# Long convolution: x turned one slot later; output projection of sublayer A with its bias as three bfloat16 rows

## The chip, the cores and the metric

The kernel runs on one core of a Trainium2 chip. The metric is the device time of one execution in microseconds (us); lower is better. The core has a matrix engine (TensorE, PE in the profile, with its weight loads as PEld), a vector engine (VectorE, DVE), a scalar engine (ScalarE, ACT), a general engine (GpSimd, POOL) and a queue that issues most transfers (SyncE, SP). Each works through its own instructions in order; semaphores tie them together.

## The reference, cut to what matters

The reference is a small network of two layers over x, 4096 rows (two sequences of 2048) of 256 numbers. Each sublayer normalizes x and adds its result to it. Eight follow each other: a scan (sublayer A), a router with slots, a doubling recurrence (sublayer B), the router again, a long convolution (sublayer C), a ternary feed-forward, attention (sublayer D), the feed-forward again.

```python
# sublayer A, behind its scan over 2048 steps
y = y * jax.nn.silu(z)
return y @ W_out + b_out
# sublayer C: 512 channels, a filter of 1024 taps each
x = _silu(xc)                       # xc: a causal filter of 4 taps over the input projection
x_f = jnp.fft.rfft(x, n=n); k_f = jnp.fft.rfft(k_ssm, n=n)
y = jnp.fft.irfft(x_f * k_f[None], n=n)[..., :Lq]
y = y + x * D_skip[None, :, None]
y = y * _silu(z)
return jnp.einsum('bhl,dh->bld', y, W_out)
```

## The kernel before

**Sublayer A** (`sublayer_a`) runs in three stages. `scan_tables` loads x in 32 tiles (`sa_xi`, L182), normalizes them and makes the tables of the scan. `scan` is the loop over 2048 steps (L410 to L488). Then comes the output projection: for each of 32 tiles of 128 rows a multiplication on DVE (L570), a bias matmul (L572: a row of ones against the row `b_out`, both f32 and one partition high), two f32 matmuls over the halves of the 256 channels (L574), and an addition to the resident x on DVE (`add_to_x`, L156). PSUM has four buffers for these products. `load_x` (L583) brings x into SBUF in eight transfers of 512 KB. The order of the instructions here is set by a scheduler, which may move them ahead on their queue when they wait for nothing and their tile's place in SBUF is free. The weights of the router, which follow, are loaded into the place of sublayer A's tiles.

**`bias_rows`** (L825) exists in the kernel before and is used by sublayer B and by the feed-forward. It splits an f32 row into three bf16 rows whose sum is the row, and puts them into the first three partitions of a tile of zeros 128 partitions high:

```python
t = pool.tile([P, n], BF16, name=name, tag=name)
V.memset(t, 0.0)
...
for k in range(3):
    piece = pool.tile([1, n], BF16, ...)
    V.tensor_copy(piece, rest)
    if k < 2:
        V.tensor_tensor(rest, rest, piece, ALU.subtract)
    nc.sync.dma_start(out=t[k : k + 1], in_=piece)
```

A matmul of a bf16 tile of ones (128 by 128) with such a tile adds the bias to every row.

**Sublayer C** (`sublayer_c`) handles its 512 channels in four blocks of 128 (e = 0 to 3). A block has 32 slots, and a slot convolves four channels (`convolve`, L1185: 72 small matmuls against a Toeplitz table). The order in this loop is written out by hand and kept. Four slots (r = 0 to 3) make a group, and a group does three things side by side:

- every slot: `load_toep` (L1109, SP) loads the table of two slots ahead into one of three buffers, which the slot before must have left; `fill_toep` fills up the next slot's table with two copies on DVE (L1117, L1119) and two on ACT (L1118, L1120); then `convolve` runs on PE.
- blocks 0 to 2 prepare the next block's input, 512 columns per group: `x_project` (slot 0, PE), `x_first` (slot 0: a copy on ACT, two instructions on DVE), `x_rest` (slot 1, two on DVE), `x_silu` (slot 2, L1164 on ACT, and a transfer by POOL), `x_turn` (slot 3, L1171: four transposes on PE, ahead of the slot's convolution), `x_keep` (slot 3, L1175: a copy on DVE, behind the slot's fill).
- blocks 1 to 3 finish the block before: `leave` (every block, slot 0), `y_load` (slot 0, POOL), `y_gate` (slot 1, PE), `y_silu` (slot 1, ACT), `y_join` (slot 2, L1220 and L1221 on DVE), `y_project` (slot 3, L1229: eight f32 instructions on PE, behind x_turn and ahead of the convolution), `y_add` (slot 3, L1237 on DVE).

Of the kernel before, what the change touches and what calls it, by code (L numbers as in the profile page):

```python
# [23 lines left out]
P = 128  # L24
B, S, D = 2, 2048, 256
# [27 lines left out]
BF16 = mybir.dt.bfloat16  # L53
# [6 lines left out]
def new(pool, shape, name, **kw):  # L60
    return pool.tile(list(shape), F32, name=name, tag=name, **kw)


class Kernel:
# [486 lines left out]
    def sublayer_a(self):  # L551
        tc, nc = self.tc, self.nc
        with ExitStack() as c:
            dp = c.enter_context(tc.tile_pool(name="a_dram", bufs=1, space=DRAM))
            kp = c.enter_context(tc.tile_pool(name="a_keep", bufs=1))
            tabd = dp.tile([96, NT], F32, name="tabd", tag="tabd")
            dtd = dp.tile([4, NT + TG, 64], F32, name="dtd", tag="dtd")
            dxd = dp.tile([4, NT + TG, 64], F32, name="dxd", tag="dxd")
            zs = new(kp, [P, 2, NT], "zs")
            y = new(kp, [P, 2, NT], "y")  # L560
            self.scan_tables(zs, dtd, dxd, tabd)
            self.scan(y, dtd, dxd, tabd)
            self.open_x()
            self.load_x(self.a["x"])
            wo = self.load(kp, "A_W_out", pat="(k p) n -> p k n", p=P)
            bo = self.load_row(kp, "A_b_out")
            pp = c.enter_context(tc.tile_pool(name="a_ps", bufs=4, space=PSUM))
            for i in range(NI):
                ts = slice(i * P, (i + 1) * P)
                nc.vector.tensor_tensor(zs[:, :, ts], zs[:, :, ts], y[:, :, ts], ALU.mult)  # L570
                ps = new(pp, [P, D], "ps_o")
                nc.tensor.matmul(ps, self.ones1, bo, start=True, stop=False)  # L572
                for k in range(2):
                    nc.tensor.matmul(ps, zs[:, k, ts], wo[:, k, :], start=False, stop=k == 1)  # L574
                self.add_to_x(i, ps)
# [496 lines left out]
    def sublayer_c(self):  # L1072
# [7 lines left out]
        tc, nc = self.tc, self.nc  # L1080
# [4 lines left out]
        with ExitStack() as c:  # L1085
# [3 lines left out]
            kp = c.enter_context(tc.tile_pool(name="c_k", bufs=1))  # L1089
# [14 lines left out]
            def load_toep(s):  # L1104
                e, g = s // 32, s % 32
                t = toeps[s] = new(kb, [P, 4, W], "toep")
                for r in range(2):
                    first = kr.offset + (e * P + 4 * g + 2 * r) * KREV
                    nc.sync.dma_start(  # L1109
                        out=t[r * (P - Q) : r * (P - Q) + Q, 2 * r : 2 * r + 2],  # L1110
                        in_=bass.AP(kr.tensor, first, [[1, Q], [KREV, 2], [1, W]]),
                    )

            def fill_toep(s):
                t = toeps[s]
                a, b = t[:, 0:2], t[:, 2:4]
                V.tensor_copy(a[Q : 2 * Q, :, 0 : W - Q], a[0:Q, :, Q:W])  # L1117
                A.copy(b[2 * Q : 3 * Q, :, Q:W], b[3 * Q : P, :, 0 : W - Q])  # L1118
                V.tensor_copy(a[2 * Q : P, :, 0 : W - 3 * Q], a[0 : 2 * Q, :, 2 * Q : W - Q])  # L1119
                A.copy(b[0 : 2 * Q, :, 3 * Q : W], b[2 * Q : P, :, Q : W - 2 * Q])  # L1120
# [13 lines left out]
            def x_project(e, ch):  # L1134
                ps = held["x"] = new(pp, [P, CH], "ps")
                for k in range(2):
                    nc.tensor.matmul(
                        ps, wi[:, k, e * P : (e + 1) * P], xT[:, k, ch * CH : (ch + 1) * CH],
                        start=k == 0, stop=k == 1,
                    )  # L1140
# [26 lines left out]
            def x_turn():  # L1167

                ps = held["t"] = new(pt, [P, 4, P], "ps_t")
                for j in range(4):  # L1170
                    nc.tensor.transpose(ps[:, j, :], held["xs"][:, j * P : (j + 1) * P], self.ident)  # L1171

            def x_keep(e, ch):
                b, i0 = ch // 4, ch % 4 * 4
                V.tensor_copy(  # L1175
                    xring[e % 2][:, :, TAPS + i0 : TAPS + i0 + 4, b], held["t"].rearrange("p j c -> p c j")
                )

            def convolve(s, ps):
                e, g = s // 32, s % 32  # L1180
                x, t = xring[e % 2], toeps.pop(s)
                for m in range(TAPS + 1):
                    for j in range(4):
                        lo = L_CONV - m * P + j // 2 * (P - Q)
                        nc.tensor.matmul(  # L1185
                            ps[j * 32 : (j + 1) * 32, g % 4, :],
                            x[:, 4 * g + j, TAPS - m : TAPS - m + NB, :].rearrange("p i b -> p (i b)"),
                            t[:, j, lo : lo + P], start=m == 0, stop=m == TAPS,
                        )

            def leave(s, ps):

                ys = new(tp, [P, 4, P], "c_ys")
                A.copy(ys, ps[:, :, ::-1])
                G.dma_start(
                    out=yd[4 * s : 4 * s + 16].rearrange("(s j) i b t -> (j i b) s t", j=4), in_=ys
                )


            def y_load(e, ch):  # L1200
                b, i0 = ch // 4, ch % 4 * 4
                yc, xs = held["yc"], held["yx"] = new(tp, [P, CH], "c_yc"), new(tp, [P, CH], "c_xs")
                G.dma_start(out=yc.rearrange("p (i t) -> p i t", t=P), in_=yd[e * P : (e + 1) * P, i0 : i0 + 4, b])
                G.dma_start(out=xs, in_=xd[e * P : (e + 1) * P, ch * CH : (ch + 1) * CH])

            def y_gate(e, ch):
                ps = held["z"] = new(pp, [P, CH], "ps")
                z0 = E * P + e * P
                for k in range(2):
                    nc.tensor.matmul(  # L1210
                        ps, wi[:, k, z0 : z0 + P], xT[:, k, ch * CH : (ch + 1) * CH], start=k == 0, stop=k == 1
                    )

            def y_silu():
                sz = held["sz"] = new(tp, [P, CH], "c_acc")
                A.activation(sz, held["z"], AF.Silu)
# [6 lines left out]
            def y_project(e):  # L1223
                yc = held["yc"]
                held["o"] = []
                for j0 in range(0, 4, 2):
                    ps = new(po, [P, 2, D], "ps_o")
                    for j in (j0, j0 + 1):
                        nc.tensor.matmul(  # L1229
                            ps[:, j - j0], yc[:, j * P : (j + 1) * P], wo[:, e, :], start=True, stop=True  # L1230
                        )
                    held["o"].append(ps)
# [18 lines left out]
            fill_toep(0)  # L1251
            x_turn()
            x_keep(0, NCH - 1)
            out = None
            for s in range(32 * E):
                e, q, r = s // 32, s % 32 // 4, s % 4
                more, done = e + 1 < E, e > 0
                if s + 2 < 32 * E:
                    load_toep(s + 2)
                if r == 0:  # L1260
                    before, out = out, new(pc, [P, 4, P], "ps_c")
                    if more:
                        x_project(e + 1, q)
                elif r == 1 and done:
                    y_gate(e - 1, q)
                elif r == 3:
                    if more:
                        x_turn()
                    if done:
                        y_project(e - 1)  # L1270
                if s + 1 < 32 * E:
                    fill_toep(s + 1)
                convolve(s, out)
                if r == 0:
                    if before is not None:
                        leave(s - 4, before)
                    if done:
                        y_load(e - 1, q)
                    if more:
                        x_first(e + 1, q)  # L1280
                elif r == 1:
                    if done:
                        y_silu()
                    if more:
                        x_rest(e + 1)
                elif r == 2:
                    if more:
                        x_silu(e + 1, q)
                    if done:
                        y_join(e - 1)  # L1290
                else:
                    if more:
                        x_keep(e + 1, q)
                    if done:
                        y_add(q)
            leave(32 * E - 4, out)
# [473 lines left out]
```

## Time and profile before

| | |
|---|---|
| time, median of 3 runs (range) | 13714.66 us (13710.65 to 13725.5) |
| the profiled execution's own time | 13713.61 us |
| its span, first to last instruction | 13711.9 us |
| busy: PE, DVE, ACT, POOL | 5477.8, 10653.5, 9294.0, 460.9 us |
| output projection of sublayer A | 10040.7 to 10142.1 us |
| convolution loop of sublayer C | 11039.8 to 11738.7 us |
| mean granted clock of PE | 0.609 of full speed |

The page gives busy times by engine, the span in 40 slices of 343 us, and the costliest groups of instructions, each with the idle time before it and what ended that. The timeline gives single instructions with start and length in us from the span's start; what stands in brackets is the idle time of the engine just before and who ended it. PEclk is the share of full speed that PE's clock was granted.

### The profile page before, as it was taken

How to read it: one execution, taken by the hardware profiler on the slowest of the kernel's cores; microseconds unless marked ns; L12 is line 12 of the kernel's file. 1: busy time of each engine (PE TensorE's matmuls, PEld its weight loads, DVE VectorE, ACT ScalarE, POOL GpSimd, SP SyncE). 2: the span in 40 equal slices, each digit the busy share in tenths (PEclk: the TensorE clock that was granted, in tenths of full speed). 3: DMA queues.
4: the chain of work that ended last, by engine and by line, in shares of the span. 5: the costliest groups of instructions: out<-in, count | busy, mean ns of one | idle time of the engine just before them, and what ended most of it. 6: DMA issues, size and time to landing. Idle time of an engine off the chain costs nothing. (4 is left out here: it accounts for less than half of the span.)

```text
span 13711.9 us, 263042 instructions
## 1 busy us (share of the span) xinstructions
PE 5477.8 (40%) x66344; PEld 3762.0 (27%) x66344; DVE 10653.5 (78%) x65491; ACT 9294.0 (68%) x45234; POOL 460.9 (3%) x528
## 2 busy tenths in 40 slices
PE   4222222222222222222222222222269867778888
PEld 2111111111111111111111111111135545644445
DVE  6888888888888888888888888888857677655555
ACT  3777777777777777777777777777735478534444
POOL 0000000000000000000000000000000001131110
PEclk6555555555555555555555555555559888889999
DMA  3000000000000000000000000000000045242210
GB/s 81 14 14 17 14 17 15 17 16 15 17 14 17 14 17 14 17 14 17 14 17 17 14 16 15 17 14 17 14 13 4 7 134 155 73 94 34 35 31 19
DMA packets 320440, 382.28 MB, mean 28 GB/s; under 512 B 207074, under 2 KB 230697, under 8 KB 317876
## 3 DMA queue, kind: packets, MB, share of 16 engines
q1 hardware_dynamic: 299444, 322.01, 10.2%
q0 software_dynamic: 17408, 42.75, 1.0%
q8 instruction: 533, 8.73, 0.3%
q14 instruction: 1007, 8.25, 0.2%
q10 hardware_dynamic: 2048, 0.53, 0.0%
HBM read 307.96 MB, written 52.46 MB: 26 GB/s over the span
## 5 line engine op out<-in xcount | busy, mean ns | idle before, releaser
L410 PE MATMUL hc<-hs,mean 128*32 128x2 f32 x16384 | 586.1, 203 | 7096.9 <-DVE hs L480 7033.2
L410 PEld LDWEIGHTS hc<-hs,mean 128*32 128x32 f32 x16384 | 410.6, 140 | 7308.9 <-DVE hs L480 7244.7
L475 DVE TENSOR_TENSOR p<-p,ir 128x64 f32<-128x64 f32 x4096 | 737.4, 221 | 1062.9 <-ACT ir L463 1062.9
L459 ACT ACTIVATE lm<-m 128x64 f32<-128x64 f32 x2048 | 466.2, 228 | 1210.2 <-DVE m L451 1210.2
L493 PE MATMUL yps<-cs,hist 128*64 128x8 f32 x8192 | 1224.9, 259 | 13.0 <-DVE hs L480 13.0
L391 ACT ACTIVATE bx<-dx,tc 128x64 f32<-128x64 f32 x4098 | 1169.4, 332 | 0.1
L1594 ACT ACTIVATE d_p<-ps_e 128x512 f32<-128x512 f32 (+3 forms) x1280 | 599.5, 537 | 754.2 <-PE ps_o L1575 534.8
L493 PEld LDWEIGHTS yps<-cs,hist 128*64 128x64 f32 x8192 | 1033.1, 218 | 45.1 <-DVE hs L480 13.4
L418 ACT ACTIVATE sq<-hc 128x2 f32<-128x2 f32 x2048 | 352.9, 172 | 795.2 <-PE hc L410 795.2
L480 DVE CUSTOM_DVE_ANT_0 hist<-p,sg 128x64 f32<-128x64 f32 x4096 | 761.0, 222 | 23.0 <-ACT rm L470 4.2
L477 DVE SCALAR_TENSOR_TENSOR p<-e,p 128x64 f32<-128x64 f32 x4096 | 738.1, 221 | 9.9 <-ACT sg L469 7.8
L442 DVE TENSOR_TENSOR p<-p,fac 128x64 f32<-128x64 f32 x4096 | 737.4, 221 | 8.9 <-DVE p L437 6.6
L444 DVE TENSOR_TENSOR p<-p,bx 128x64 f32<-128x64 f32 x4096 | 722.2, 218 | 2.6
L439 ACT ACTIVATE fac<-ngd,ci 128x64 f32<-128x64 f32 x2048 | 711.8, 348 | 1.0 <-DVE p L436 1.0
L436 DVE SCALAR_TENSOR_TENSOR p<-hist,ea 128x64 f32<-128x64 f32 x2048 | 459.7, 224 | 323.3 <-ACT ea L429 323.3
L429 ACT ACTIVATE ea<-ex 128x64 f32<-128x64 f32 x2048 | 524.3, 256 | 99.6 <-DVE ex L424 7.0
L1587 PE MATMUL ps_e<-d_qt,d_kt 128*128 128x512 f32 (+3 forms) x1280 | 556.4, 444 | 43.0 <-ACT d_p L1594 34.6
L472 ACT ACTIVATE ld<-e 128x64 f32<-128x64 f32 x2048 | 548.0, 268 | 0.0
L473 ACT ACTIVATE k<-rm 128x64 f32<-128x64 f32 x2048 | 545.0, 266 | 0.0
L410 PE MATMUL hd<-hs,mean 128*32 128x2 f32 x16384 | 543.7, 193 | 0.0
L1544 PE MATMUL ps_m<-d_kt,d_qt 128*128 128x512 f32 (+3 forms) x1280 | 499.3, 436 | 101.3 <-DVE d_part L1549 40.3
L432 PE MATMUL hd<-ident,ci 128*1 128x1 f32 x4096 | 386.7, 163 | 357.2 <-DVE ex L424 303.4
(453 smaller groups left out, 22720.5 us busy)
## 6 DMA issues: line engine op xcount, KB each, us to landing
toep<-in_C_krev SPq DMA_DIRECT2D x256, 312.0 KB, 5.5
ng<-dtd SPq DMA_DIRECT2D x258, 256.0 KB, 3.4
dx<-dxd SPq DMA_DIRECT2D x258, 256.0 KB, 3.9
d_kt<-d_kd SPq DMA_DIRECT2D x128, 128.0 KB, 4.1
d_qt<-d_qd SPq DMA_DIRECT2D x128, 128.0 KB, 3.7
y<-ys SPq DMA_DIRECT2D x512, 8.0 KB, 1.9
c_xd<-c_xs POOLq DMA_DIRECT2D x32, 256.0 KB, 2.6
c_yd<-c_ys POOLq DMA_DIRECT2D x32, 256.0 KB, 4.3
```

Source lines behind the costliest of these rows:

```text
L391: A.activation(bx[o][:, k2], tg[j][2][:, k], AF.Identity, scale=tg[j][0][:, k2, k : k + 1], bias=0.0 if k2 else SMALL,)
L410: nc.tensor.matmul(out[r : r + 32], mean[:, r : r + 32], hs[i], start=True, stop=True)
L439: A.activation(fac, ngd, AF.Exp, scale=ci)
L442: V.tensor_tensor(p[:, k2], p[:, k2], fac, ALU.mult)
L444: V.tensor_tensor(p[:, k2], p[:, k2], bx[o][:, k2], ALU.add)
L472: A.activation(ld, e, AF.Ln, scale=-1.0, bias=1.0)
L475: V.tensor_tensor(p[:, k2], p[:, k2], ir, ALU.mult)
L477: V.scalar_tensor_tensor(p[:, k2], e, -1.0, p[:, k2], ALU.add, ALU.mult)
L480: V.tensor_tensor_reduce(out=hn[:, k2], in0=p[:, k2], in1=sg, scale=-1.0, scalar=0.0 if k2 else J * SMALL, op0=ALU.mult, op1=ALU.add, accu ...
L493: nc.tensor.matmul(yps[:, k, :], hist[g][:, k, k2], tg[g][3][:, k2, k], start=k2 == 0, stop=k2 == 1)
L1587: nc.tensor.matmul(s[:, q0:], ks[kt // 4][:, hh, kt % 4 * P : (kt % 4 + 1) * P], q[:, hh, q0:], start=True, stop=not diag,)
L1594: A.activation(pr[:, q0:], s[:, q0:], AF.Exp, scale=0.25)
```

## The change

Two edits, apart from each other.

In `sublayer_a` the bias is made into three bf16 rows by `bias_rows` ahead of the scan, together with a bf16 tile of ones; the projection's bias matmul takes these two. In `sublayer_c`, x_turn and x_keep of a group no longer stand in its slot 3 but in slot 0 of the next group, one after the other: x_turn ahead of x_project on PE, x_keep ahead of that slot's fill on DVE. What is still to be turned is remembered in `waiting`.

```diff
             y = new(kp, [P, 2, NT], "y")
+            ones_b = kp.tile([P, P], BF16, name="a_ones", tag="a_ones")
+            nc.vector.memset(ones_b, 1.0)
+            bo = self.bias_rows(kp, self.load_row(kp, "A_b_out"), "a_bo", D)
             self.scan_tables(zs, dtd, dxd, tabd)
             self.scan(y, dtd, dxd, tabd)
             self.open_x()
             self.load_x(self.a["x"])
             wo = self.load(kp, "A_W_out", pat="(k p) n -> p k n", p=P)
-            bo = self.load_row(kp, "A_b_out")
...
-                nc.tensor.matmul(ps, self.ones1, bo, start=True, stop=False)
+                nc.tensor.matmul(ps, ones_b, bo, start=True, stop=False)
...
-            out = None
+            out = waiting = None
...
                     before, out = out, new(pc, [P, 4, P], "ps_c")
+                    if waiting:
+                        x_turn()
+                        x_keep(*waiting)
+                        waiting = None
                     if more:
                         x_project(e + 1, q)
                 elif r == 1 and done:
                     y_gate(e - 1, q)
-                elif r == 3:
-                    if more:
-                        x_turn()
-                    if done:
-                        y_project(e - 1)
+                elif r == 3 and done:
+                    y_project(e - 1)
...
                     if more:
-                        x_keep(e + 1, q)
+                        waiting = (e + 1, q)
```

## The prediction

> **What bounds the kernel now.** I read the page first. The span is 13711.9 us, and slices 2 to 29 (of 343 us each) hold the scan of sublayer A, in which PE waits 7,033 us for `hs`. The change touches neither that loop's instructions nor their order on any engine. So only what lies around it can move: the start, the output projection behind the loop, and sublayer C.
>
> ```profile
> span 13711.9 us, 263042 instructions
> PEclk6555555555555555555555555555559888889999
> L410 PE MATMUL hc<-hs,mean 128*32 128x2 f32 x16384 | 586.1, 203 | 7096.9 <-DVE hs L480 7033.2
> ```
>
> Next the timeline of one output tile of the projection, and of the value tiles of sublayer B (L957, L960), which have the form that the change gives the projection (four f32 instructions and one bf16 bias, 128x256).
>
> ```profile
> 10060.77 2.08 PE L574 MATMUL ps_o<-w_A_W_out,zs 128*128 128x256 f32 x4
> 10062.78 1.22 PE L572 MATMUL ps_o<-w_A_b_out,ones 1*128 1x256 f32 x2
> 10063.92 2.08 PE L574 MATMUL ps_o<-w_A_W_out,zs 128*128 128x256 f32 x4
> ...
> 10350.81 0.27 PE L960 MATMUL ps<-b_bv,b_ones 128*128 128x256 bf16 x1
> 10350.92 1.03 PE L957 MATMUL ps<-w_B_attn_W,b_xT 128*128 128x256 f32 x4
> 10351.78 0.27 PE L960 MATMUL ps<-b_bv,b_ones 128*128 128x256 bf16 x1
> ```
>
> A projection tile comes every 10063.92 - 10060.77 = 3.15 us, a value tile every 0.97 us. Three stretches say why. Columns: length, PE, PEld, DVE, ACT, POOL busy, granted clock, DMA share, GB/s. They are the projection, the L721 matmuls of the router, and the value tiles.
>
> ```profile
> 10044.00:10140.00 96.00, 96.00 (x183) 50.94 (x184) 34.99 (x124) 0.62 (x3) 0.00 (x0) 0.50 0.00 1
> 10270.00:10288.00 18.00, 18.00 (x45) 13.87 (x45) 8.76 (x22) 0.00 (x0) 0.00 (x0) 0.50 0.00 1
> 10346.00:10376.00 30.00, 30.00 (x156) 24.07 (x155) 13.93 (x32) 0.00 (x0) 0.00 (x0) 1.00 0.00 1
> ```
>
> PE is busy throughout in all three, yet the first two are granted half the clock. They are the ones whose matmuls feed few rows: one row in 1.14 of each 3.15 us (L572), 64 rows in L721; L957 and L960 feed 128 always.
>
> Last, one group of four slots in the convolution (channel block 1; slots 0 and 3 start at 11318.23 and 11337.29), and its waits over blocks 1 and 2.
>
> ```profile
> 11318.23 2.17 PE L1185 MATMUL ps_c<-toep,c_x 128*32 128x128 f32 x72
> 11327.77 2.21 ACT L1118 COPY toep<-toep 32x2432 f32<-32x2432 f32 x1 [1.34 <-DMA toep<-in_C_krev]
> 11330.01 2.11 ACT L1120 COPY toep<-toep 64x2304 f32<-64x2304 f32 x1
> 11332.15 0.63 ACT L1164 ACTIVATE c_xs<-c_acc 128x512 f32<-128x512 f32 x1
> 11332.83 1.12 PE L1171 MATMUL ps_t<-ident,c_xs 128*128 128x128 f32 x4 [4.69 <-ACT c_xs L1164]
> 11333.74 3.62 PE L1229 MATMUL ps_o<-w_C_W_outT,c_yc 128*128 128x256 f32 x8
> 11337.29 2.33 PE L1185 MATMUL ps_c<-toep,c_x 128*32 128x128 f32 x72
> ...
> PE ps_t L1171 <- ACT c_xs L1164: 77.9, 15, 7.0
> ACT toep L1118 <- DMA toep<-in_C_krev: 37.6, 17, 3.6
> ```
>
> The slots turn in a ring: convolve 3, x_project, convolve 0, the table for slot 3 loads into the buffer that convolve 0 has freed, ACT fills it, x_silu, x_turn, y_project, convolve 3.
>
> **The change, part by part.**
>
> *Bias as bf16 rows.* Per tile two one-row f32 instructions go and one 128-row bf16 one comes. The row L957/L960 gives 0.97 us per tile at full clock; doubled, 1.95 at half. Whether the clock rises decides. [...]
>
> Does DVE keep up? Behind the loop it has 32 multiplications and 32 additions at 0.34 us from start to start (0.42 busy), and, ahead of the last addition, some 24 statistics at 0.33 and 35 small ones at 0.1: 33 us from 10040.5, close to PE. With the two in step I put the last addition at 10077 instead of 10142.1 (start of PE at 10040.7): **-65 us** (half clock: -38). All behind it follows: SP issues the router's weights only on the last addition (10141.71), PE then waits 15.9 us for them, and DVE normalizes at 10170. DVE's remaining statistics fit into that.
>
> *The load of x is moved.* In the changed program the eight transfers of x (512 KB each) no longer stand at the front of SP's queue but behind the loop, ahead of the router's weights; the additional tiles of the bias (3.3 KB per partition) presumably take x's free place. So x loads now from about 10040.5, when the engines leave the loop, and the first addition waits for it.
>
> ```profile
> L583 SPq DMA_DIRECT2D x<-in_x x8: 432/506/2020, 11.9 to 25.8; - x8
> ...
> DMA to landing us min/median/max: 6.0/8.2/9.2
> ```
>
> These landed in 6 to 9 us amid other loads; DVE first multiplies for 11 x 0.34 = 3.7 us, and PE has four banks, 4 x 1.95 = 7.8 us. First landing near 10046: about 1 us of DVE, inside the 10077. Four tiles then need 512 KB every 3.9 us = 134 GB/s, against 225 GB/s in slices of the start. If the first landed at 10050, +4 us. The router's weights queue behind them but wait for the last addition anyhow. The start loses 8 transfers that nothing waited for, also nothing.
>
> *Bias pieces at the start.* SP now issues b_out's row first and three pieces between the weights, each on DVE. Four issues at 0.5 us, plus a wait for row and cast (row about 2 us, copy and cast 0.27 each): SP reaches the first sa_xi load 3 us later than 4.36. DVE waited for it 4.45 us (to 6.61) and is then the bound of the tables, so 3 us late is 3 us: **+3** (0 to +5). The eight small DVE instructions and two memsets lie in that wait.
>
> *x one slot later.* x_turn leaves the ring between silu and y_project, and stands in slot 0 between convolve 3 and x_project. x_keep goes with it, on DVE ahead of the two fill copies for slot 1. Groups of blocks 1 and 2 take 24.1 us now: by the timeline, the last convolve 3 of block 0 starts at 11191.16 and the last of block 2 at 11576.73, 385.6/16. The ring: 2.3 + 1.85 + 2.2 + 7.6 (end of convolve 0 to ACT's fill, mean of the 16) + 4.35 + 0.65 + 4.6 (turn and y_project) + 0.5 of hand-overs = 24.05. After the change three rings compete:
> - load: 2.3 + x_turn 0.9 + 1.9 + 2.2 + 7.6 + 4.35 + 0.4 = 19.7; with the longest of the 16 loads (9.4), 21.5.
> - DVE: convolve 3 at 2.3, x_turn 0.9, x_keep 0.7, fill 2.8, accumulate 1.55, fill 2.8, taps 1.55, fill 2.8, join 1.55, y_project 1.9 to 3.3, hand-overs 0.8 = 19.7 to 21.1.
> - ACT: four fills at 4.35, four others at 0.6 = 19.8.
>
> Three near-equal rings with shared waits come out a little over the longest: 21.5 us, so 16 x 2.6 = **-42 us**, ends -10 (23.5) and -60 (20.3). Conv 1 stands behind x_keep: convolve 3 + 0.9 + 0.7 + 2.8 = 4.4 us, while PE has turn, x_project, convolve 0, y_gate = 6.9 us of its own; so no loss while that cover stands (in block 0, without y_gate, 5.0, barely). Block 0 (19.5 us a group, ACT 97% busy) gains about 2 us in all. At the three borders convolve 0 needs x_keep: hidden by x_project twice, 1 us once.
>
> *Sum* against the profiled execution, 13713.6 us (1.7 outside the span): -65 + 3 - 42 - 2 + 1 = -105, 13608.6; the median is 1.05 above that execution: **13610 us**.
>
> **Rivals.**
> 1. The clock stays at half in the projection: 13610 + 27 = 13637. [...] Against it: the stretches above.
> 2. The convolution's wait only changes its name: load or DVE holds the group at 24 us, 13652. For it: 37.6 us of waits for the table stand there already, and the y transfers fall into the same slot. Against it: blocks 0 and 3 run at 19.5 and 19.7 us with the same tables.
> 3. The projection waits for x: transfers at 60 GB/s would take 70 us, the whole gain of the projection, 13675. Against it: 225 GB/s at the start, with nothing else on the queues here.
> 4. Slower: x_keep at DVE's head. DVE stops until PE has done convolve 3 and x_turn; three fills, accumulations, taps and join follow in order. It decides when the DVE ring exceeds 24.1 + 62/16 = 28 us, 7 us over my sum; each us beyond costs 16. Against it: DVE is busy 266.7 of 358.2 us there.
>
> **How the numbers follow.** Main case 0.63, rival 1 0.13, rival 2 0.15, rival 3 0.04, rival 4 0.02, rest 0.03. Main case alone: 13585 to 13635 (C's ends, x, start). Range 13582 to 13658, which takes in rivals 1 and 2. A measurement here tells 0.2% (27 us) from no change: 13687 is the line. Faster 0.94, within 0.04, slower 0.02.
>
> **What would show it.** [...] SP: eight x loads just behind the loop, DVE's wait for them near 1 us. Start: first statistics near 9.6. Convolution: no long wait of `ps_t` for `c_xs`, groups at 21.5, ACT's busy share in blocks 1 and 2 from 80% to 90%. Wrong if the clock stays 0.50, if DVE's fill waits for x_keep, or if table loads stretch.

## The result and the profile after

The changed kernel takes 13611.76 us (median of 6 runs, 13606.84 to 13617.74) against 13710.6 for the kernel before on the same chip (6 runs, 13710.17 to 13725.5): ratio 0.9926, interval 0.9913 to 0.9939. The forecast was 13610. The profiled execution took 13606.84 us, 106.8 less than that of before, where the sum said 105. The total fits better than its terms do, so it is the terms that follow.

The page of the changed kernel, its span and its row of granted clock:

```profile
span 13605.1 us, 263019 instructions
PEclk7555555555555555555555555555569888889999
```

Laid side by side at landmarks that both traces have (first and last scan step, first and last matmul of the projection, first value tile of sublayer B, the slots of sublayer C), the two profiled executions differ so:

| stretch | before, us | after, us | difference | said |
|---|---|---|---|---|
| start, to the first scan step | 370.5 | 371.5 | +1.0 | +3 |
| scan loop | 9664.0 | 9661.3 | -2.7 | 0 |
| projection, PE first to last | 101.0 | 33.5 | -67.5 | -65 |
| from there to sublayer B's value tiles | 204.3 | 200.9 | -3.4 | 0 |
| convolution, block 0 | 151.3 | 147.7 | -3.7 | -2 |
| blocks 1 and 2 | 385.6 | 352.7 | -32.9 | -42 |
| block 3 | 159.4 | 164.1 | +4.7 | 0 (borders +1) |
| all other stretches | | | -2.3 | 0 |

**The projection.** The timeline just behind the loop, with the transfers of x, the first addition and two tiles further on:

```profile
10038.61 10.84 SPq L585 DMA_DIRECT2D x<-in_x  x8
10043.37 0.75 DVE L156 TENSOR_TENSOR x<-x,ps_o 128x256 f32<-128x256 f32 x2 [0.80 <-DMA x<-in_x]
...
10047.96 0.27 PE L574 MATMUL ps_o<-a_bo,a_ones 128*128 128x256 bf16 x1
10048.07 1.03 PE L576 MATMUL ps_o<-w_A_W_out,zs 128*128 128x256 f32 x4
10048.38 0.41 DVE L156 TENSOR_TENSOR x<-x,ps_o 128x256 f32<-128x256 f32 x1
10048.94 0.27 PE L574 MATMUL ps_o<-a_bo,a_ones 128*128 128x256 bf16 x1
```

A tile comes every 10048.94 - 10047.96 = 0.98 us where it was 3.15. x is issued behind the loop, and DVE's first addition waits 0.80 us for it. The windows of the projection and of the router's 64-row matmuls (columns as in the prediction: length, busy time of PE, PEld, DVE, ACT, POOL, granted clock, DMA share, GB/s):

```profile
10044.00:10072.00 28.00, 28.00 (x146) 22.42 (x144) 27.45 (x112) 0.42 (x2) 0.00 (x0) 1.00 0.36 114
10197.00:10222.00 25.00, 24.76 (x60) 19.20 (x61) 12.30 (x30) 0.00 (x0) 0.00 (x0) 0.50 0.00 0
```

The projection has the full clock (1.00, PE busy 28.00 of 28 us); the router's stage, which the change does not touch, still has half with PE as busy (0.50, 24.76 of 25). DVE is busy 27.45 of 28 us in the projection: it is as near to being the bound as PE.

**The convolution.** One group of block 1, from convolve 0 on; behind it the longest waits of PE and DVE in blocks 1 and 2 (total us, times, longest):

```profile
11341.57 2.17 PE L1187 MATMUL ps_c<-toep,c_x 128*32 128x128 f32 x72
11345.64 0.77 DVE L1157 TENSOR_SCALAR c_acc<-c_xi,w_C_conv_w,w_C_conv_b 128x512 f32<-128x512 f32 x1 [1.95 <-ACT c_xi L1154]
11350.17 3.87 PE L1187 MATMUL ps_c<-toep,c_x 128*32 128x128 f32 x72 [2.40 <-DVE toep L1121]
11355.41 0.69 DVE L1223 TENSOR_TENSOR c_yc<-c_yc,c_acc 128x512 f32<-128x512 f32 x1
11356.20 2.53 PE L1231 MATMUL ps_o<-w_C_W_outT,c_yc 128*128 128x256 f32 x8 [2.16 <-issue]
...
PE ps_o L1231 <- issue: 37.9, 12, 3.9
DVE c_x L1177 <- PE ps_t L1173: 36.7, 16, 3.2
PE ps_c L1187 <- DVE toep L1121: 21.2, 17, 3.3
PE ps_o L1231 <- DVE c_yc L1223: 18.5, 4, 6.0
DVE c_acc L1157 <- ACT c_xi L1154: 14.1, 8, 3.3
```

The wait of `ps_t` for `c_xs` (77.9 us before) is gone from the list. In its place PE stands at y_project: 37.9 + 18.5 = 56.4 us, 3.5 a group. The row put down to "issue" belongs with the `c_yc` row: y_project begins at 11356.20, just behind the end of DVE's `c_yc` (11355.41 + 0.69), and in all 16 groups it begins 0.06 to 0.10 us behind that end. Groups take 352.7/16 = 22.04 us.

### The profile page after: what moved, and what is told of

Same layout as the page of the kernel before. It is cut to its first block, busy times and chain, and to the rows that moved or that the text cites. A ratio compares the mean times of both kernels' runs of the same rounds, so it can differ in the third digit from the quotient of the medians.

```text
span 13605.1 us, 263019 instructions
## 1 busy us (share of the span) xinstructions
PE 5403.6 (40%) x66312; PEld 3727.9 (27%) x66312; DVE 10649.4 (78%) x65499; ACT 9293.9 (68%) x45234; POOL 458.8 (3%) x528
```

## The experiments

Where a few us matter, the stretches of the table above are compared and not the medians. Over the 14 traces of this case the loop, whose instructions are the same in all, took 9657.5 to 9675.4 us.

**One part at a time.** `turn_only` is the kernel before with the edit of sublayer C:

```diff
                 if r == 0:
                     before, out = out, new(pc, [P, 4, P], "ps_c")
+                    if waiting:
+                        x_turn()
+                        x_keep(*waiting)
+                        waiting = None
...
-                elif r == 3:
-                    if more:
-                        x_turn()
-                    if done:
-                        y_project(e - 1)
+                elif r == 3 and done:
+                    y_project(e - 1)
...
-                        x_keep(e + 1, q)
+                        waiting = (e + 1, q)
```

> The kernel before with only the edit of the convolution: x_turn and x_keep one slot later, the projection as it was. Theory from the two traces: the landmarks of the changed kernel give -3.7 us in block 0, -32.9 in blocks 1 and 2, +4.7 in block 3 and -2 behind it, together -34: 13676 to 13678 us. The prediction's own step said -42 - 2 + 1 = -43: 13667. Rival: the +4.7 of block 3 belongs to chance in the loads of the tables and not to the edit; then it is absent here, block 3 stays near 159 us, and the time is 13672. All three have the projection's tiles at 3.15 us and the loop beginning as before.

Measured: 13680.04 us, ratio 0.998 (0.9972 to 0.9988). Blocks 1 and 2 took 352.0 us, groups of 22.00; block 0 149.7, block 3 170.5. The gain in blocks 1 and 2 is therefore the edit's, and its size repeats: three traces with exactly this order (this one, the changed kernel and router_rows) have 352.0, 352.7 and 352.8 us, and those with the small variants keep_late and keep_late_first 348.6 to 349.2, while five traces with the old order have 385.6, 384.2, 380.0, 373.9 and 383.6. Against the mean of those five (381.5) the edit is worth 29 us; the 385.6 from which the prediction started was the longest of them. Block 3 says nothing: it lasted 159.4 to 168.7 us in the five traces with the old order and 159.8 to 170.5 with the new (`load_more`, below, apart).

`bias_only` is the kernel before with the edit of the bias:

```diff
+            ones_b = kp.tile([P, P], BF16, name="a_ones", tag="a_ones")
+            nc.vector.memset(ones_b, 1.0)
+            bo = self.bias_rows(kp, self.load_row(kp, "A_b_out"), "a_bo", D)
...
-            bo = self.load_row(kp, "A_b_out")
...
-                nc.tensor.matmul(ps, self.ones1, bo, start=True, stop=False)
+                nc.tensor.matmul(ps, ones_b, bo, start=True, stop=False)
```

> The kernel before with only the bias of the output projection as three bfloat16 rows in a tile of 128; the convolution as it was. Theory: projection -67.5 us, router -3, start +1 to +2.5: 13710.6 - 69 = 13642 us, last addition 34 us behind the loop, granted clock 1.00 there, groups in blocks 1 and 2 of the convolution still 24.1 us. The prediction's step: -65 + 3 = -62, 13649. Rival: the loop (9,660 us long), which was 2.7 us shorter in the trace of the changed kernel than in that of before, gave part of the gain as a consequence of the edit; then it is shorter here too. If that was chance, the loop's length here has no fixed sign.

Measured: 13633.29 us, ratio 0.9943 (0.9926 to 0.996). Projection 34.0 us, groups of blocks 1 and 2 at 24.01. The loop took 9667.2 us, longer than before's 9664.0: its -2.7 in the changed kernel was chance. The two parts together, -28.9 and -75.7 against the kernel before of their chip, give -104.6 where both at once gave -98.8; they add up within the scatter of the runs.

**What lifts the clock** from half to full. A full matmul is here one that feeds 128 rows. `bias_f32_rows` keeps the number and the type of the instructions and changes only the rows:

```diff
-            bo = self.load_row(kp, "A_b_out")
+            ones_f = new(kp, [P, P], "a_onesf")
+            nc.vector.memset(ones_f, 1.0)
+            bo = new(kp, [P, D], "a_bof")
+            nc.vector.memset(bo, 0.0)
+            nc.sync.dma_start(out=bo[0:1], in_=self.a["A_b_out"].rearrange("(o n) -> o n", o=1))
...
-                nc.tensor.matmul(ps, self.ones1, bo, start=True, stop=False)
+                nc.tensor.matmul(ps, ones_f, bo, start=True, stop=False)
```

> The kernel before with the bias still in float32, but as a tile of 128 rows (row 0 the bias, the rest zero) against 128 rows of ones: the same six float32 instructions per tile as before, with 128 rows fed in all of them. It loads x at the front of the queue as before. Theory of rows fed: the clock goes to 1.00 after the first 5 us; a tile takes 6 x 0.214 = 1.28 us, the projection 5 + 30 x 1.28 = 43 us instead of 101: -57 us, 13653. Rival, the type and number of instructions hold the clock: it stays 0.50, a tile takes 6 x 0.43 = 2.57 us, the projection 82 us: -19, 13692.

Measured: 13654.17 us, ratio 0.9958 (0.9941 to 0.9974), projection 43.4 us. Its timeline and its window:

```profile
10070.30 1.03 PE L578 MATMUL ps_o<-w_A_W_out,zs 128*128 128x256 f32 x4
10071.17 0.59 PE L576 MATMUL ps_o<-a_bof,a_onesf 128*128 128x256 f32 x2
10071.60 1.03 PE L578 MATMUL ps_o<-w_A_W_out,zs 128*128 128x256 f32 x4
...
10059.00:10095.00 36.00, 36.00 (x169) 31.68 (x168) 30.42 (x115) 0.63 (x3) 0.00 (x0) 1.00 0.00 1
```

Six float32 instructions as before, tiles of 1.30 us, clock 1.00. Neither the type nor the number held it at half (0.50 before); with 127 rows of zeros it was at 1.00.

`bias_three_rows` takes the bfloat16 rows of bias_only, but only the three that hold something:

```diff
-                nc.tensor.matmul(ps, ones_b, bo, start=True, stop=False)
+                nc.tensor.matmul(ps, ones_b[:3], bo[:3], start=True, stop=False)
```

> As bias_only, but the bias matmul takes only the three rows that hold something (3 of 128 rows of the tile), in bfloat16. [...] Rival, any matmul of few rows among the others holds the clock: 0.50, tile 1.95 us, 62 us in all, 13642 + 29 = 13671.

Measured: 13647.02 us, ratio 0.9956 (0.9939 to 0.9972). The clock rose, but the projection took 42.3 us and not 34:

```profile
10046.03 1.13 PE L576 MATMUL ps_o<-w_A_W_out,zs 128*128 128x256 f32 x4
10047.09 0.28 PE L574 MATMUL ps_o<-a_bo,a_ones 3*128 3x256 bf16 x1
10047.30 1.13 PE L576 MATMUL ps_o<-w_A_W_out,zs 128*128 128x256 f32 x4
10048.37 0.28 PE L574 MATMUL ps_o<-a_bo,a_ones 3*128 3x256 bf16 x1
...
10044.00:10080.00 36.00, 36.00 (x143) 21.69 (x142) 29.42 (x111) 0.51 (x3) 0.00 (x0) 1.00 0.28 89
```

Tiles of 1.27 us at full clock, 0.30 more than with 128 rows. From one instruction's start to the next it is 0.21 us from the bias to the first full matmul (0.11 in the changed kernel), 0.32 from there to the second (0.22) and 0.31 from the last to the bias (0.22). About 0.1 us goes in each of these three places: where the rows change, and once more between the two full matmuls just behind a change. The old tile shows the same at half clock: in the trace of before the starts from 10060.77 on lie 0.59, 0.42, 0.43, 0.57, 0.58 and 0.56 us apart (four full ones, then the two of the bias). Six instructions at 0.427 us make 2.56 of its 3.15 us, and the other 0.59 went at the two changes and just behind them, about 0.15 in each place. The run doesn't settle whether fewer rows lift the clock, since PE begins with eight full matmuls in a row, and the clock had risen by the time the mixed tiles came (the first, at 10042.22, takes 1.13 us as those at 1.00 do).

`four_first` puts a longer row of full matmuls, sixteen of them, ahead of the old, one-row tiles:

```diff
-            for i in range(NI):
-                ...
-                nc.tensor.matmul(ps, self.ones1, bo, start=True, stop=False)
-                for k in range(2):
-                    nc.tensor.matmul(ps, zs[:, k, ts], wo[:, k, :], start=False, stop=k == 1)
-                self.add_to_x(i, ps)
+            for group in [range(4)] + [[i] for i in range(4, NI)]:
+                ...
+                    for k in range(2):
+                        nc.tensor.matmul(ps, zs[:, k, ts], wo[:, k, :], start=k == 0, stop=False)
+                for i, ps in zip(group, banks):
+                    nc.tensor.matmul(ps, self.ones1, bo, start=False, stop=True)
+                for i, ps in zip(group, banks):
+                    self.add_to_x(i, ps)
```

> The kernel before, its one-row float32 bias kept, but in the first four tiles of the projection the sixteen full matmuls run back to back and the four biases follow; the other 28 tiles have the bias behind their own matmuls. So the first 6.8 us feed 128 rows without a gap, and the rest feeds them in about half the time, as before. Theory, a full stretch lifts the clock and less keeps it: 1.00 from about 5 us on and up to the end, tiles of 1.28 + 0.4 for the changes of rows = 1.7 us, the projection 28 x 1.7 + 9 = 57 us instead of 101: -44, near 13666. [...]

Measured: 13667.28 us, ratio 0.9964 (0.995 to 0.9978), projection 55.3 us. Timeline and window:

```profile
10060.78 1.13 PE L576 MATMUL ps_o<-w_A_W_out,zs 128*128 128x256 f32 x4
10061.84 0.69 PE L578 MATMUL ps_o<-w_A_b_out,ones 1*128 1x256 f32 x2
10062.47 1.13 PE L576 MATMUL ps_o<-w_A_W_out,zs 128*128 128x256 f32 x4
...
10055.00:10104.00 49.00, 49.00 (x178) 28.43 (x176) 32.53 (x117) 0.63 (x3) 0.00 (x0) 1.00 0.00 1
```

These are the old instructions, one-row bias and all, 1.69 us a tile instead of 3.15, at 1.00 to the end. All 128 rows are fed in 4 x 0.216 = 0.86 us of the 1.69, 51%, and that kept the clock, while at half clock 4 x 0.427 = 1.71 of 3.15 us, 54%, never lifted it. So as a share of the time, lifting and keeping would be two conditions. Counted as full instructions per us they need not be two: the tiles of bias_f32_rows lifted the clock at 1 / 0.427 = 2.34 a us, four_first kept it at 4 / 1.69 = 2.37, and the old tiles did not lift it at 4 / 3.15 = 1.27. One bound between 1.27 and 2.34 would fit all three (an estimate from these tiles); no run separates the two readings.

`router_rows` tries the same cause elsewhere, where PE has no changes of rows at all:

```diff
             for b in range(B):
-                rows = slice(b * 64, (b + 1) * 64)
+                half = new(tp, [P, D], "s_half")
+                V.memset(half, 0.0)
+                V.tensor_copy(half[b * 64 : (b + 1) * 64, :], svo[b * 64 : (b + 1) * 64, :])
...
-                        ps[:, :D], alphaT[rows, i * P : (i + 1) * P], svo[rows, :], start=True, stop=True
+                        ps[:, :D], alphaT[:, i * P : (i + 1) * P], half, start=True, stop=True
```

> The changed kernel, with the router's last 32 tiles (64 rows, 25 us of busy PE at 0.50 in every trace so far, and no change of rows between the matmuls) taken over all 128 rows: svo is copied into a tile whose other half is zero, and alphaT is used whole. As many matmuls, with as many columns; only the rows fed double. Theory of rows fed: after about 5 us the clock goes to 1.00 and a tile takes 0.43 us instead of 0.85: 27.3 us become about 16, -11: near 13600. Rival, what held the clock was not the rows (the change of rows from one matmul to the next, or something in this stage): 0.50 throughout, 0.85 us a tile, no gain.

Measured: 13587.05 us, ratio 0.9905 (0.9888 to 0.9921). The stage in this kernel, and a window in it:

```profile
10203.95 15.47 PE L725 MATMUL ps<-s_half,alphaT 128*128 128x256 f32 x64 [0.84 <-DVE s_half L722]
...
10207.00:10219.00 12.00, 12.00 (x57) 10.47 (x56) 11.69 (x28) 0.00 (x0) 0.00 (x0) 1.00 0.00 0
```

The 32 tiles take 15.5 us instead of 26.8 in the changed kernel; the clock rose 2.9 us after the first of them. The expectation forgot that the router runs twice: from the end of the projection to the first value tile 200.9 us became 189.5, and from there to the convolution, the second use, 694.0 became 679.0.

**What holds the groups of the convolution.** `keep_late` takes x_keep from the head of DVE's slot 0:

```diff
                     if waiting:
                         x_turn()
-                        x_keep(*waiting)
-                        waiting = None
...
                     fill_toep(s + 1)
+                if r == 0 and waiting:
+                    x_keep(*waiting)
+                    waiting = None
                 convolve(s, out)
```

> The changed kernel, with x_keep on DVE behind the two fill copies for slot 1 instead of ahead of them (x_turn stays in slot 0). In blocks 1 and 2 DVE waited 36.7 us, 2.3 a group, at x_keep for x_turn. Theory, DVE's ring holds the groups at 22.0: that wait goes, DVE's ring falls to about 19.8 and ACT's (19.8) is the next, groups of 20.3 us, 16 x 1.7 = -27: near 13584. Rival, the ring of the table's load holds them: groups stay at 22.0 us, the waits change names, time as the changed kernel (13611). A value between says that DVE's next wait (for ACT's c_xi) takes part of it.

Measured: 13603.46 us, ratio 0.9918 (0.9902 to 0.9935). Blocks 1 and 2 took 349.1 us, groups of 21.82. Of 2.3 us a group that DVE no longer waits, 0.2 arrived, and this row of its waits says where the rest went:

```profile
DVE c_acc L1157 <- ACT c_xi L1154: 40.6, 16, 4.8
```

It was 14.1 us. DVE came to the next hand-over sooner and waited for ACT there. `keep_late_first` then has ACT copy c_xi sooner:

```diff
                 if r == 0:
+                    if more:
+                        x_first(e + 1, q)
                     if before is not None:
                         leave(s - 4, before)
                     if done:
                         y_load(e - 1, q)
-                    if more:
-                        x_first(e + 1, q)
```

> As keep_late, and in slot 0 ACT copies c_xi (x_first) before it takes the finished group from PSUM (leave) instead of after, 0.57 us sooner for DVE, which waits for it 14.1 us in blocks 1 and 2 of the changed kernel. Theory, DVE and ACT hold the groups in turn: 0.3 to 0.5 us a group below keep_late, ACT above 95% busy, near 20 us: -5 to -8 against keep_late, near 13577. Rival, loads: no difference from the changed kernel.

Measured: 13602.47 us, ratio 0.9917 (0.99 to 0.9933), groups of 21.83: nothing on top of keep_late. Taking these two waits out of DVE's order hardly shortens the group.

`load_more` adds to each load of a table a third transfer, which brings a quarter of its bytes again, to a place where the second has just written them:

```diff
             for r in range(2):
                 ...
+            nc.sync.dma_start(
+                out=t[P - Q : P, 2:3], in_=bass.AP(kr.tensor, first, [[1, Q], [KREV, 1], [1, W]])
+            )
```

> The changed kernel, with one more transfer per slot of the convolution, which repeats a quarter of the table that is loaded anyhow (156 KB beside two of 312 KB); nothing else. It lengthens the load in the ring of load by about a quarter, 1.9 us of the 7.6 from the end of convolve 0 to ACT's fill, and leaves DVE's and ACT's rings as they are. Theory, the load's ring holds the groups of blocks 1 and 2 at 22.0 us: they become 23.5 to 24, +24 to +32 us there and +13 in block 3 if it holds that too, 13645 to 13655. Rival, DVE's and ACT's waits for each other hold them: the load has slack, groups within 0.5 us of 22.0, under 13622.

Measured: 13702.26 us, ratio 0.9993 (0.9983 to 1.0003): all of the change's gain is gone. Groups of blocks 1 and 2 take 399.1/16 = 24.95 us, and blocks 0 and 3 (169.5 and 192.0 us) are about 3 us a group longer too. That is nearly 3 us a group where 1.5 to 2 were expected, and in every block. The longest wait for a table over blocks 1 and 2, and SP's queue over two slots there (L1111 the first two transfers, L1115 the third):

```profile
ACT toep L1123 <- DMA toep<-in_C_krev: 75.7, 47, 7.8
...
11209.86 0.78 SPq L1111 DMA_DIRECT2D toep<-in_C_krev  x2
11214.77 0.32 SPq L1115 DMA_DIRECT2D toep<-in_C_krev  x1
11216.00 0.78 SPq L1111 DMA_DIRECT2D toep<-in_C_krev  x2
11220.79 0.32 SPq L1115 DMA_DIRECT2D toep<-in_C_krev  x1
11221.28 0.78 SPq L1111 DMA_DIRECT2D toep<-in_C_krev  x2
```

The edit did more than lengthen a load. SP issued the third transfer only when the second had landed (0.02 us behind the landing in all 16 slots of these blocks where the trace has it), 4.33 to 7.99 us behind its issue. The next table's transfers stood behind it on SP's queue: in 54 of 64 slots they followed within 0.6 us, as at 11221.28, where in the changed kernel at least 2.75 us lie between a table's last transfer and the next table's first. So the loads went out one table after the other, and SP's queue set the pace, 6.2 us a slot. Whether a quarter more bytes would have had room, the question of this run, stays open. Whether the loads held the groups at 22 us is answered by the next kernel, which loads what keep_late_first loads.

`y_late`, on keep_late_first, moves y_project as the change moved x_turn:

```diff
                     if more:
                         x_project(e + 1, q)
+                    if due:
+                        y_project(due[0])
...
-                elif r == 3 and done:
-                    y_project(e - 1)
...
                     if before is not None:
                         leave(s - 4, before)
+                    if due:
+                        y_add(due[1])
+                        due = None
...
                     if done:
-                        y_add(q)
+                        due = (e - 1, q)
             leave(32 * E - 4, out)
+            y_project(due[0])
+            y_add(due[1])
```

> As keep_late_first, and y_project with y_add goes the same way as x_turn: out of slot 3 into slot 0 of the next group. In blocks 1 and 2 PE still waits 56 us, 3.5 a group, ahead of y_project for c_yc, with convolve 3 behind it: the place where it waited for c_xs before the change. Theory, that wait took over from the one removed and holds the groups: groups of 20.3 us, -1.5 x 16 = -24 against keep_late_first (13602), and block 3 shorter by up to 8: 13570 to 13580. Rival, the load or ACT holds them at 21.8: PE waits as long for toep instead, within 5 us of 13602.

Measured: 13577.93 us, ratio 0.9902 (0.9885 to 0.9918). Blocks 1 and 2 took 323.0 us, groups of 20.19, and the rest of the convolution stood where it was (block 3 161.5). The window over blocks 1 and 2, and PE's longest wait there:

```profile
11113.70:11436.70 323.00, 259.53 (x4920) 197.19 (x4920) 274.70 (x285) 311.14 (x194) 47.90 (x64) 0.91 0.68 181
...
PE ps_c L1187 <- DVE toep L1121: 56.0, 30, 3.8
```

PE no longer waits at y_project. It waits as long for the tables (56.0 us), but ACT is now busy 311.14 of 323.0 us, 96%, so little of that wait could still be gained. Against keep_late_first the groups fell by 1.64 us, with as many bytes to load: it was not the size of the loads that had held them near 22 us, nor the two waits of DVE, but PE's stop at y_project, with convolve 3 behind it, the same stop at the same place as x_turn's before. y_add, which needs y_project, moved with it; no run moves one without the other.

**Both together.** `best` is keep_late_first with the router's edit; `both_late` is y_late with it.

> keep_late_first and router_rows together, on the changed kernel. Both add up: -9 and -24.5 from 13611.8, near 13578. If both are chance of the loads and of the granted clock, it stands with router_rows at 13587.

> y_late with the router's last tiles over all 128 rows (in both of its uses), as in router_rows. Theory, the two gains have nothing in common and add up: y_late measured 13578 us, router_rows 24.7 below the changed kernel (13587.05 against 13611.76): near 13554, groups of blocks 1 and 2 at 20.2 us. Rival, as in the kernel best, which came out at 13588 where 13578 was expected, a part is lost to the lengths that differ from run to run (loop, block 3): 13560 to 13575.

Measured: best 13588.49 us, ratio 0.9908 (0.9891 to 0.9924), no better than router_rows alone. In their traces blocks 1 and 2 are 4.2 us shorter (348.6 against 352.8), but the stretch from the projection to the first value tile is 5.0 longer (194.5 against 189.5). Of these, 1.6 lie in the router's last tiles, where the clock rose 6.2 us after the first and not 2.9. both_late 13551.31 us, ratio 0.9884 (0.9867 to 0.99): both gains in full, 60 us below the changed kernel and the fastest here.

## Why the prediction was right, and where it was not

- **The projection, -65.** Right, in mechanism and in size (-67.5). The last addition was put at 10077, 36 us behind the loop, and came at 10072.54, 33.8 us behind DVE's first multiplication. The clock rose 4.3 us after PE's first matmul. That it went with the rows fed and not with how busy PE is, bias_f32_rows and router_rows show: with rows of zeros it was 1.00 with PE busy 36.00 of 36 us and 12.00 of 12, where it had been 0.50 with PE as busy (96.00 of 96 us in the projection of before, 24.76 of 25 in the router of the changed kernel). The -65 counts a first stretch at half clock; no run shows the length taken for it, and what the runs showed in its place is 3.2 to 5.8 us from the first matmul to the rise, in the twelve traces in which the projection's clock rose. Rival 1 (half clock) fell: the clock was 1.00.
- **What the prediction left out here.** It read the stage as a share of rows. four_first shows that such a share alone does not decide: the old instructions keep a clock that they don't lift. A change of order alone would have given 45.7 of the 67.5 us.
- **x behind the loop, 1 us.** Right: 0.80 us, one wait. Rival 3 fell.
- **Bias pieces, +3.** The first issue of sa_xi came 2.5 us later (6.89), the first statistics at 9.05 (said: 9.6). By the first scan step it is +2.1: mean 372.3 us over the ten traces with the pieces, 370.2 over the four without.
- **x one slot later, -42.** The term that was mis-sized: -32.9 in this trace, 29 against the mean of the old order. The load's ring was taken as the longest, with the DVE ring at 19.7 to 21.1 beside it. What held the group was PE at y_project, waiting for DVE's join with convolve 3 behind it; with the same loads, y_late's groups take 20.19 us. The working has y_project in DVE's ring, but as work and without that wait, and it leaves out DVE's own wait for c_xi (14.1/16 = 0.9 us a group). How much of the 22.0 each of the two makes stays open: keep_late_first was to shorten the second and moved nothing. The prediction looked for no long wait of `ps_t` for `c_xs`, rightly, and didn't ask what stands at the same place next: 56.4 us at y_project, 3.5 a group, which y_late removed for 1.6 us a group beyond keep_late_first. Rival 2, that the wait only changes its name, was right by half: its sum (24 us) was wrong, its mechanism was there, with another wait than the table's.
- **x_keep hidden.** Nearly: moving it gave 0.2 us a group. Rival 4 had no part.
- **The sum.** The convolution gave 11 us less than its terms (-32 over its four blocks, -43 said). What made it up was the projection (-2.5), the start (-2), and 8.4 us in stretches that the change doesn't touch and whose lengths differ from trace to trace (loop -2.7, router -3.4, rest -2.3). The mechanisms were right, the closeness of 13610 to 13611.76 owes something to chance.

## What to carry to other kernels

A busy PE was not a PE at full clock here (96.00 of 96 us at 0.50): look at the granted clock of the stage, and where it is half, at the rows that its matmuls feed; rows of zeros cost no matmul time here (0.27 us for a bias matmul of 128 rows, 0.28 for one of three) and nearly halved a stage (26.8 us to 15.5 in the router), and sixteen full matmuls ahead brought the projection from 101 us to 55.3. When an instruction that waits is moved to a later place in an in-order queue, look for the next one at the same place that waits for the same chain, and move it too: here the second move brought almost as much as the first. Compare a stage with its own spread over several traces before building a sum on one. And when a transfer is added to try out a load, look at when it is issued: load_more's had to wait for the transfer before it (4.33 to 7.99 us), and so tried the queue and not the load.

## What was not expected of the hardware

- The clock stayed at 1.00 through 49 us in which 128 rows were fed about half the time (four_first, 51% of a tile), and never rose in 101 us of the same instructions that began without a full stretch (54%). As a share of the time, lifting would need more than keeping; as full instructions per us one bound could serve for both (2.34 lifted, 2.37 kept, 1.27 did not lift; an estimate from these tiles).
- Two changes a tile between few and 128 rows cost 0.30 us at full clock (bias_three_rows, 1.27 against 0.97), about 0.1 us of it behind the change, between two full matmuls. PE is shown as busy in it (36.00 of 36 us).
